# An involution loop in steps of two tile rows, with longer runs of each kind of matmul and the norm parameters in other PSUM buffers

## The chip, the cores and the metric

The kernel runs on one core of one Trainium2 chip. The metric is the device time in microseconds (us), as the median of several executions; the three of the kernel before lie between 2418.53 and 2431.75 us. Times inside an execution come from one profiled execution, whose span is 2421.5 us. PE is TensorE, DVE VectorE, ACT ScalarE, POOL GpSimd and SP SyncE, which here issues the DMAs.

## The reference, cut to what matters

The input is x, 8 images of 256 channels and 56 x 56 pixels, in float32. Two layers follow each other, each with a residual:

```python
x = x + involution(group_norm(x))            # layer 0
x = x + ternary_conv_block(group_norm(x))    # layer 1

def involution(x):                           # K = 7, 16 groups
    ker = w_span @ (w_reduce @ x + b_reduce) + b_span    # per pixel: 16 groups x 49 taps
    out[c, y, x] = sum over the 49 taps of ker[group of c, tap, y, x] * x_padded[c, y + ky, x + kx]
```

Layer 1 makes ternary weights of w1 and w2, and does convolution, batch norm, relu, convolution, batch norm, a sum and a relu. The change touches layer 0 alone.

## The kernel before, in words

**Stages.** A start-up of about 205 us loads the weights, quantizes the weights of layer 1 and prepares image 0. Then comes the loop of the involution, to 1244 us. Two convolution phases follow, and a last stage that sums and stores.

**Tiling of the involution.** An image is cut into 4 quarters of 64 channels (`quarters`, 32 in all); the two halves of the image's height lie on partitions 0 to 63 and 64 to 127. A half is 10 tile rows of 7 tiles, and a tile is 3 x 8 pixels (the tenth row has one line of pixels, so 8 instead of 24). For each tile the 49 taps are written as a matrix from the 9 x 14 = 126 pixels around it to its 24 pixels, and the involution of the tile is a matmul with that matrix. So three kinds of PE work belong to a tile row:

- *Application*, `apply_row` (L704, tile `pa`): 28 fp32 matmuls of 32 columns, each of which the profile shows as 2, so 56. `pick_out` then takes the result out of PSUM: ACT (L716), DVE (L717), and POOL adds it to x (L720).
- *Matrices*, `generate` (L671, tile `pg`): a quarter needs 14 units, each for 2 to 4 of the 24 pixel places and two groups (`UNITS`; 8 to 16 matmuls in the profile). A unit takes one tile of the pool `ps_p`, which has 2 buffers of two banks. Units of four places have one or two places taken out by ACT (L675, two calls a place), and DVE takes out the rest (L680), after ACT, because both work on the same PSUM tile. The matrices of quarter m + 1 are made while quarter m is applied.
- *Transposes*, `transpose_q` (L638, tile `ptq`, 3 matmuls): the pixels of three of the row's seven tile columns, normalized by POOL (`surround`), are transposed and copied by ACT (L641) beside the other four, which `load_q` brings from DRAM. Those four were made for the next image in strips (`prep`: POOL, then 4 transposes `pt`, L605, an ACT copy, L608, and a store).

`ptq` and `pt` share 2 PSUM buffers of the pool `ps_a`, and `pa` has 2 more: with the 2 x 2 banks of `ps_p` that is 8 banks.

**Order.** The loop is written out by hand. One turn is one tile row, and `pin` keeps each engine's instructions in the order of the text. A turn issues transfers, `apply_row`, the loads of four rows ahead, the transposes of two rows ahead (`QLEAD`), statistics on DVE, `pick_out`, one or two units of matrices (`PER_ROW`, none in the tenth row), a half step of a strip, and on even rows a part of `surround`.

**Norm parameters.** Once per image, in three turns, `params` makes the group norm's scale and shift of the next image: two small matmuls (`gnp`), a chain of tiny DVE instructions with one ACT square root, a scaled copy of the reducing weights, and 8 small matmuls (`br`). Its PSUM tiles come from `ps_p`, the pool of the matrices. `reduce` (tile `pk`, L538) then applies the reducing weights, in the turns that make the last units of an image.

```python
PER_ROW = (2, 1, 2, 1, 2, 1, 2, 1, 2, 0)
...
        row = apply_row(b, c, a, ty)
        prefetch()
        if m * TY + ty + QLEAD < len(rows):
            transpose_q(*rows[m * TY + ty + QLEAD])
...
        pick_out(b, c, ty, *row)
        for _ in range(PER_ROW[ty]):
            next(gen, None)
```

Of the kernel before, what the change touches and what calls it, by code (L numbers as in the profile page):

```python
# [15 lines left out]
P = 128  # L16
# [62 lines left out]
def involution_tri_block_kernel(  # L79
# [61 lines left out]
    def group_norm_params(mv, dst, psum_tile, name):  # L141


        n = mv.shape[1]
        ps = psum_tile(f"gnp_{name}")
        nc.tensor.matmul(ps[:, :2 * n], grp_sb, mv.rearrange("p n s -> p (n s)"),
                         start=True, stop=True)
        yield
        gm = small.tile([P, n, 2], F32, tag=f"gn_gm{n}", name=f"gm_{name}")
        nc.vector.tensor_copy(gm.rearrange("p n s -> p (n s)"), ps[:, :2 * n])  # L150
        d = small.tile([P, n], F32, tag=f"gn_d{n}", name=f"d_{name}")
        nc.vector.tensor_tensor(d, mv[:, :, 0], gm[:, :, 0], ALU.subtract)
        nc.vector.tensor_tensor(d, d, d, ALU.mult)
        ps2 = psum_tile(f"gnp2_{name}")
        nc.tensor.matmul(ps2[:, :n], grp_sb, d, start=True, stop=True)
# [5 lines left out]
        nc.vector.scalar_tensor_tensor(dst[:, :, 1], gm[:, :, 0], -1.0, rs, ALU.mult, ALU.mult)  # L161
# [273 lines left out]
    with ExitStack() as ph1:  # L435
# [30 lines left out]
        def params(b):  # L466


            dst = small.tile([P, NCQ, 2], F32, tag="gn1", name=f"gn1_{b}")
            yield from group_norm_params(mvs.pop(b), dst, ps_flat, f"a{b}")  # L470
            ps = ps_flat(f"br_{b}")
            for c in range(NCQ):
                nc.vector.tensor_scalar(
                    wrn[:, c, :].rearrange("p (i r) -> p i r", i=2),
                    wr[:, c, :].unsqueeze(1).to_broadcast([P, 2, CR]),
                    dst[:, c, 0:1], None, ALU.mult)
                for i in range(2):
                    nc.tensor.matmul(ps[i * CR:(i + 1) * CR, :1], wr[:CH, c, :], dst[:CH, c, 1:2],
                                     start=(c == 0), stop=(c == NCQ - 1))
# [102 lines left out]
        def prep(b):  # L582

            for c in range(NCQ):
                d = xt_d[b % 2][c][:]

                def store(src, row, o=None, d=d):

                    n = src.shape[0]
                    if o is None:
                        src, to = src.rearrange("p k c -> p (k c)"), [[1, RP]]
                    else:
                        to = [[P, NK], [1, CH]]
                    nc.sync.dma_start(
                        bass.AP(d.tensor, d.offset + row * QX * RP + (o or 0), [[RP, n]] + to), src)

                for s in range(HH // SR):
                    spread(xn, xs[b, c][:, s * SR * W:(s + 1) * SR * W], 0, NK,  # L600
                           prm[b][:, c, 0:1], prm[b][:, c, 1:2])
                    yield
                    pt = ps_a.tile([P, 512], F32, tag="pt", name=f"pt_{b}_{c}_{s}")
                    for k in range(NK):
                        nc.tensor.transpose(pt[:NSP, k * P:(k + 1) * P],  # L605
                                            xn[:, k].rearrange("p r x -> p (r x)"), ident_sb)
                    stg = work.tile([P, NK, P], F32, tag="stg", name=f"stg_{b}_{c}_{s}")
                    nc.scalar.copy(stg[:NSP].rearrange("p k c -> p (k c)"), pt[:NSP, :RP])  # L608
                    tasks.append(lambda stg=stg, s=s: store(stg[:NSP], PAD + s * SR))

                    e = PAD * QX
                    if s == 0:
                        tasks.append(lambda stg=stg: store(stg[:e, :, CH:], PAD + HH, 0))
                    elif s == HH // SR - 1:
                        tasks.append(lambda stg=stg: store(stg[NSP - e:NSP, :, :CH], 0, CH))
                    yield


        tasks = []
# [13 lines left out]

        def transpose_q(b, c, ty):

            pt = ps_a.tile([P, 512], F32, tag="pt", name=f"ptq_{b}_{c}_{ty}")
            for k in range(NX):
                nc.tensor.transpose(  # L638
                    pt[:NQ, k * P:(k + 1) * P],
                    xe[c % 2][:, k, PY * ty:PY * ty + QY].rearrange("p r x -> p (r x)"), ident_sb)  # L640
            nc.scalar.copy(loads[b, c, ty][:NQ, NK:].rearrange("p k c -> p (k c)"),  # L641
                           pt[:NQ, :NX * P])
# [94 lines left out]

        def gn2_stats(b, c, ty):

            if ty == 1:  # L740
# [36 lines left out]
            reduce(0, py)  # L777
        for _ in prep(0):
            transfer(len(tasks))
        apool = ph1.enter_context(tc.tile_pool(name="apool", bufs=1))  # L780

        def matrices(m):
# [11 lines left out]


        quarters = [(b, c) for b in range(B) for c in range(NCQ)]


        X_AT = (0, 1, 4, 5, 7, 8, 14, 15)
        STRIPS_AT = 23  # L800
        for _ in range(NQB):
            prefetch()
        for _ in surround(0, 0):
            pass
        rows = [(b, c, ty) for b, c in quarters for ty in range(TY)]
        for k in rows[:QLEAD]:
            transpose_q(*k)
        pin(start=True)
        last = None
        strips = iter(())  # L810
        for m, (b, c) in enumerate(quarters):
            a = a_next
            gen = iter(())
            if m + 1 < len(quarters):
                a_next = matrices(m + 1)
                gen = generate(*quarters[m + 1], a_next)
                around = surround(*quarters[m + 1])
            more = b + 1 < B
            for ty in range(TY):
                r = c * TY + ty  # L820

                if last is not None and ty in (2, 3):
                    store_x1(*last, ty - 2)
                elif more and r in X_AT:
                    load_x(b + 1, X_AT.index(r) // 2, X_AT.index(r) % 2)
# [7 lines left out]
                if more and r >= 20:  # L833
                    if r == 20:
                        norm = params(b + 1)
                    next(norm, None)
                if ty == 1 and last is not None:
                    gn2_stats(*last, TY)
                elif ty >= 2:
                    gn2_stats(b, c, ty - 1)  # L840
                if more and 4 <= r < 20:
                    gn1_stats(b + 1, (r - 4) // NCB, (r - 4) % NCB)
# [3 lines left out]
                if more and r == STRIPS_AT:  # L846
                    strips = prep(b + 1)
# [121 lines left out]
```

## Time and profile before

| | |
|---|---|
| device time, median of 3 | 2423.54 us |
| PE busy in the profiled execution | 1885.9 us (78%) |
| DVE busy | 1671.0 us (69%) |
| ACT busy | 1261.0 us (52%) |
| POOL busy | 592.9 us (24%) |
| involution loop | 205 to 1244 us |
| its `pg`, `pa`, `ptq` matmuls (L671, L704, L638) | 460.9, 270.4 and 178.6 us busy |

A line of groups in the profile gives the source line, the engine and operation, what is written and read with its shape, the number of instructions, busy time, the mean of one, and the engine's idle time just before them with what ended most of it. Matmuls overlap, so their busy times are longer than the distance between their starts. A "timeline" lists merged runs of instructions: start, duration, engine, line, operation, count, and in brackets the idle time before with its releaser. "issue" there is idle time for which the profile shows no awaited event.

### The profile page before, as it was taken

Reading aid. Unit: us, or ns where it says so; the run is one execution under the profiler, and the core shown is the slowest. Engines: PE = TensorE matmul, PEld = TensorE weight load, DVE = VectorE, ACT = ScalarE, POOL = GpSimd, SP = SyncE. Lnnn points to the kernel's source line nnn. Section 1 sums busy time; section 2 is a strip of 40 time slices with the busy share of each in tenths; the row PEclk is TensorE's granted clock in tenths of the full one; section 3 lists DMA queues with packets and bytes.
Section 4 is the critical chain, followed back from the end, with each engine's and each line's share of the span. In section 5 each row is a group of like instructions: output and inputs, shape, how many; then the busy total and the mean of one; then the engine's idle time right before and its main releaser. Section 6 shows DMA issues by size and latency. Waiting matters only on the chain.

```text
span 2421.5 us, 72092 instructions
## 1 busy us (share of the span) xinstructions
PE 1885.9 (78%) x31080; PEld 1711.2 (71%) x31080; DVE 1671.0 (69%) x2570; ACT 1261.0 (52%) x2404; POOL 592.9 (24%) x1325
## 2 busy tenths in 40 slices
PE   3419898989899898989968999999499999980000
PEld 2217777777777777777858999999499999980000
DVE  6277465564746466574649999999599999974444
ACT  1105454545545454555645667666466677653333
POOL 2404463545546364554630000000000000000000
PEclk8559999999999999999988999999799999995555
DMA  4426363654636364553553233222432233229998
GB/s 155 152 99 177 106 198 109 182 151 144 187 110 206 90 198 137 160 173 107 161 185 149 109 132 137 112 109 106 176 123 109 109 136 136 109 111 430 430 430 377
DMA packets 124441, 406.46 MB, mean 168 GB/s; under 512 B 25694, under 2 KB 32220, under 8 KB 115420
## 3 DMA queue, kind: packets, MB, share of 16 engines
q1 hardware_dynamic: 117664, 360.89, 43.5%
q10 hardware_dynamic: 6460, 40.97, 4.2%
q8 instruction: 244, 4.00, 0.7%
q14 instruction: 73, 0.60, 0.1%
HBM read 259.33 MB, written 142.48 MB: 166 GB/s over the span
## 4 chain that ended last, share of the span: by engine, by line
PE 41%; DMA 10%; DVE 2%; ACT 1%; issue 1%; SPq 0%; POOL 0%; ACTq 0%; DVEq 0%
PE c L388 35%; DMA y1f<-y1d 3%; PE pg L671 3%; DMA out_y<-x1f 2%; DMA x1f<-x1d 2%; PE pa L704 2%; DVE x1f L899 1%; PE ptq L638 1%; DMA y2f<-y2d 1%; DMA y1d<-y 1%; DMA wq<-wqd 1%; PE pk L538 0%; PE pt L605 0%; ACT a L675 0%; DVE a L680 0%
## 5 line engine op out<-in xcount | busy, mean ns | idle before, releaser
L388 PE MATMUL c<-pl,wq 128*128 128x392 f32 x4608 | 857.3, 348 | 51.3 <-ACT pl L294 32.0
L388 PEld LDWEIGHTS c<-pl,wq 128*128 128x128 f32 x4608 | 855.4, 189 | 53.1 <-ACT pl L294 32.8
L680 DVE TENSOR_TENSOR a<-pg,bt 126x756 f32<-126x756 f32 (+3 forms) x640 | 393.8, 656 | 283.2 <-ACT a L675 225.7
L671 PE MATMUL pg<-kr,wl 64*126 64x140 f32 (+1 forms) x6144 | 460.9, 293 | 56.8 <-DVE a L680 32.5
L671 PEld LDWEIGHTS pg<-kr,wl 64*126 64x126 f32 x6144 | 394.8, 194 | 112.0 <-issue 70.3
L704 PE MATMUL pa<-a,q 126*32 126x48 f32 x17920 | 270.4, 208 | 71.5 <-DMA q<-xtd 44.5
L641 ACT COPY q<-ptq 126x384 f32<-126x384 f32 x320 | 153.0, 478 | 314.0 <-issue 171.0
L675 ACT ACTIVATE a<-pg,bt 126x126 f32<-126x126 f32 x768 | 242.5, 475 | 136.0 <-PE pg L671 136.0
L704 PEld LDWEIGHTS pa<-a,q 126*32 126x32 f32 x17920 | 221.7, 111 | 128.5 <-issue 89.4
L720 POOL TENSOR_TENSOR x<-x,inv 128x168 f32<-128x168 f32 x320 | 165.5, 517 | 577.4 <-DVE inv L717 557.0
L717 DVE SCALAR_TENSOR_TENSOR inv<-pa,half_sb,inv 128x168 f32<-128x168 f32 x320 | 118.6, 371 | 213.3 <-ACT inv L716 212.2
L294 ACT CAST pl<-r 128x812 fp32r<-128x812 f32 x192 | 162.4, 867 | 153.0 <-DVE r L289 136.4
L351 ACT ACTIVATE dummy<-y,nc 128x1568 f32<-128x1568 f32 x128 | 205.3, 1604 | 15.6 <-DVE y L374 14.3
L295 DVE TENSOR_TENSOR pl<-r,pl 128x812 fp32r<-128x812 f32 x192 | 186.3, 996 | 30.6 <-ACT pl L294 29.7
L275 POOL MEMSET xp<- 128x116 f32 x32 | 6.3, 196 | 817.7 <-DVE a L289 817.6
L561 POOL TENSOR_SCALAR xn<-x,gn 128x224 f32<-128x224 f32 (+2 forms) x384 | 184.2, 500 | 29.1 <-PE pt L605 18.5
L638 PE MATMUL ptq<-ident_sb,xe 128*126 128x128 f32 x960 | 178.6, 296 | 9.4 <-ACT stg L608 7.0
L561 POOL TENSOR_SCALAR xe<-x,gn 128x168 f32<-128x168 f32 (+2 forms) x384 | 160.3, 437 | 19.9 <-DVE gn L161 19.9
L139 DVE BATCH_NORM_STATS2 st<-x 128x6 f32<-128x392 f32 x256 | 138.0, 555 | 9.9 <-DMA x<-in_x 9.3
L608 ACT COPY stg<-pt 98x512 f32<-98x512 f32 x128 | 79.9, 624 | 122.0 <-PE pt L605 61.6
L716 ACT ACTIVATE inv<-pa,half_sb 128x168 f32<-128x168 f32 x320 | 126.9, 397 | 1.9 <-PE pa L704 1.8
L638 PEld LDWEIGHTS ptq<-ident_sb,xe 128*126 128x126 f32 x960 | 101.3, 143 | 29.7 <-ACT stg L608 7.2
(134 smaller groups left out, 1740.2 us busy)
## 6 DMA issues: line engine op xcount, KB each, us to landing
q<-xtd SPq DMA_DIRECT2D x320, 252.0 KB
raw<-x1d SPq DMA_DIRECT2D x32, 812.0 KB
raw<-y1d SPq DMA_DIRECT2D x32, 812.0 KB
x<-in_x SPq DMA_DIRECT2D x64, 392.0 KB
xtd<-stg SPq DMA_DIRECT2D x128, 196.0 KB
x1d<-x SPq DMA_DIRECT2D x64, 392.0 KB
y1d<-y SPq DMA_DIRECT2D x32, 784.0 KB
y2d<-y SPq DMA_DIRECT2D x32, 784.0 KB
```

Source lines behind the costliest of these rows:

```text
L294: nc.scalar.copy(hi, r)
L295: nc.vector.tensor_tensor(lo, r, hi.bitcast(F32), ALU.subtract)
L351: nc.scalar.activation(dummy, y[:, to], f, bias=shift[:, to:to + 1], accum_out=stats[:, to, j, n:n + 1])
L388: nc.tensor.matmul(ps[:, to, :NM], wq[:, k, t, dx, to * P:(to + 1) * P], part[:, t, :, dx:dx + W], start=(c == 0), stop=(c == last))
L561: nc.gpsimd.tensor_scalar(dst[:, i - d - k0:f - d - k0, :, x0:x0 + n], v[:, i:f, :, j0:j0 + n], scale, bias, ALU.mult, ALU.add)
L638: nc.tensor.transpose(pt[:NQ, k * P:(k + 1) * P], xe[c % 2][:, k, PY * ty:PY * ty + QY].rearrange("p r x -> p (r x)"), ident_sb)
L641: nc.scalar.copy(loads[b, c, ty][:NQ, NK:].rearrange("p k c -> p (k c)"), pt[:NQ, :NX * P])
L671: nc.tensor.matmul(dst, wl[rows, c, gp, o:o + NQ], kr[py][rows, px, :], start=True, stop=True)
L675: nc.scalar.activation(whole[:, g0 + i, p0 + j], ps[:NQ, i, j * nt:(j + 1) * nt], AF.Identity, bias=bt[:, c, g0 + i, p0 + j:p0 + j + 1])
L680: nc.vector.tensor_tensor(dst[:, g0:g0 + 2, p0:p0 + nv].rearrange("q g p t -> q g t p"), ps[:NQ, :, t0 * nv:t1 * nv].rearrange("q i (t p) ...
L704: nc.tensor.matmul(ps[o:o + 32, k * 2 * n:(k + 1) * 2 * n], q[:NQ, k, o:o + 32], av[:, t + k, g * 2 * n:(g + 1) * 2 * n], start=True, stop ...
L720: nc.gpsimd.tensor_tensor(xv, xv, iv.rearrange("p t (y x) -> p y t x", x=PX), ALU.add)
```

## The change

A turn of the loop becomes a step of two tile rows. In a step PE first applies both rows, then makes three units of matrices (two in the fifth step of a quarter, `PER_STEP`), then does the transposes of two rows, now four rows ahead, and then those of a strip. So each kind of matmul comes in a run twice as long, and PE changes between kinds less often, which is what it is for. `pick_out` of both rows, DVE's statistics and the loads move with it; a strip is now one turn of its generator and not two.

The norm parameters take their PSUM tiles from the two buffers of the transposes (`ps_one`) and not from those of the matrices, and `params` is cut into six parts, two to a step, so that a part's DVE work stands behind the step's other DVE work. The buffer counts of all pools stay as they were, and so do all instructions of layer 1.

```diff
-PER_ROW = (2, 1, 2, 1, 2, 1, 2, 1, 2, 0)
+PER_STEP = (3, 3, 3, 3, 2)
+NS = len(PER_STEP)
 NQB = 4
-QLEAD = 2
...
         nc.vector.tensor_tensor(d, d, d, ALU.mult)
+        yield
         ps2 = psum_tile(f"gnp2_{name}")
...
+        def ps_one(name):
+            return ps_a.tile([P, 512], F32, tag="pt", name=name)
...
-            yield from group_norm_params(mvs.pop(b), dst, ps_flat, f"a{b}")
-            ps = ps_flat(f"br_{b}")
+            yield from group_norm_params(mvs.pop(b), dst, ps_one, f"a{b}")
             for c in range(NCQ):
                 nc.vector.tensor_scalar(
...
-                for i in range(2):
-                    nc.tensor.matmul(ps[i * CR:(i + 1) * CR, :1], wr[:CH, c, :], dst[:CH, c, 1:2],
-                                     start=(c == 0), stop=(c == NCQ - 1))
...
             prm[b], prm_edge[b] = dst, edge
+            yield
+            ps = ps_one(f"br_{b}")
+            for c in range(NCQ):
+                for i in range(2):
+                    nc.tensor.matmul(ps[i * CR:(i + 1) * CR, :1], wr[:CH, c, :], dst[:CH, c, 1:2],
+                                     start=(c == 0), stop=(c == NCQ - 1))
             yield
...
-            for ty in range(TY):
-                r = c * TY + ty
...
+            for s in range(NS):
+                n = c * NS + s
...
                 transfer(2)
-                row = apply_row(b, c, a, ty)
-                prefetch()
-                if m * TY + ty + QLEAD < len(rows):
-                    transpose_q(*rows[m * TY + ty + QLEAD])
...
+                step = [(ty, apply_row(b, c, a, ty)) for ty in (2 * s, 2 * s + 1)]
+                for _ in step:
+                    prefetch()
...
+                next(norm, None)
...
-                pick_out(b, c, ty, *row)
-                for _ in range(PER_ROW[ty]):
+                for ty, row in step:
+                    pick_out(b, c, ty, *row)
+
+                for _ in range(PER_STEP[s]):
                     next(gen, None)
...
+                for k in rows[(m * NS + s) * 2 + NQB:(m * NS + s) * 2 + NQB + 2]:
+                    transpose_q(*k)
                 next(strips, None)
-                if ty % 2 == 0 and m + 1 < len(quarters):
-                    next(around)
+                for _ in range((2, 2, 1, 0, 0)[s]):
+                    next(around, None)
+                next(norm, None)
                 pin()
```

More of the change, by code (lines that the diff above doesn't have):

```diff
@@ L602, in prep @@
                     yield
-                    pt = ps_a.tile([P, 512], F32, tag="pt", name=f"pt_{b}_{c}_{s}")
+                    pt = ps_one(f"pt_{b}_{c}_{s}")
                     for k in range(NK):
@@ L608, in prep @@
                     nc.scalar.copy(stg[:NSP].rearrange("p k c -> p (k c)"), pt[:NSP, :RP])
[L609 removed]
+                    tasks.append(lambda stg=stg, s=s, store=store: store(stg[:NSP], PAD + s * SR))
                     e = PAD * QX
                     if s == 0:
[L613 removed]
+                        tasks.append(lambda stg=stg, store=store: store(stg[:e, :, CH:], PAD + HH, 0))
                     elif s == HH // SR - 1:
[L615 to L616 removed]
+                        tasks.append(lambda stg=stg, store=store: store(stg[NSP - e:NSP, :, :CH], 0, CH))
         tasks = []
@@ L634, in transpose_q @@
         def transpose_q(b, c, ty):
-            pt = ps_a.tile([P, 512], F32, tag="pt", name=f"ptq_{b}_{c}_{ty}")
+            pt = ps_one(f"ptq_{b}_{c}_{ty}")
             for k in range(NX):
@@ L738, in gn2_stats @@
         def gn2_stats(b, c, ty):
-            if ty == 1:
+            if (b, c) not in gst:
                 gst[b, c] = (small.tile([P, NCB, 6], F32, tag="gn_st2", name=f"st2_{b}_{c}"), 0)
@@ L779, in involution_tri_block_kernel @@
             transfer(len(tasks))
+        transfer(len(tasks))
         apool = ph1.enter_context(tc.tile_pool(name="apool", bufs=1))
@@ L796, in involution_tri_block_kernel @@
         quarters = [(b, c) for b in range(B) for c in range(NCQ)]
-        X_AT = (0, 1, 4, 5, 7, 8, 14, 15)
-        STRIPS_AT = 23
+        rows = [(b, c, ty) for b, c in quarters for ty in range(TY)]
+        STATS_AT, PARAMS_AT, STRIPS_AT = 2, 10, 12
         for _ in range(NQB):
@@ L804, in involution_tri_block_kernel @@
             pass
-        rows = [(b, c, ty) for b, c in quarters for ty in range(TY)]
-        for k in rows[:QLEAD]:
+        for k in rows[:NQB]:
             transpose_q(*k)
@@ L809, in involution_tri_block_kernel @@
         last = None
-        strips = iter(())
+        strips = norm = iter(())
         for m, (b, c) in enumerate(quarters):
             a = a_next
-            gen = iter(())
+            gen = around = iter(())
             if m + 1 < len(quarters):
@@ L818, in involution_tri_block_kernel @@
             more = b + 1 < B
-            for ty in range(TY):
-                r = c * TY + ty
[L822 to L825, printed above, removed]
-                transfer(2)
-                row = apply_row(b, c, a, ty)
-                prefetch()
-                if m * TY + ty + QLEAD < len(rows):
-                    transpose_q(*rows[m * TY + ty + QLEAD])
[L833 to L837, printed above, removed]
-                    gn2_stats(*last, TY)
[L839 to L842, printed above, removed]
-                pick_out(b, c, ty, *row)
-                for _ in range(PER_ROW[ty]):
+            for s in range(NS):
+                n = c * NS + s
+                if more and n == PARAMS_AT:
+                    norm = params(b + 1)
+                if more and n == STRIPS_AT:
+                    strips = prep(b + 1)
+                if more and n < 2 * NCQ:
+                    load_x(b + 1, n // 2, n % 2)
+                transfer(2)
+                step = [(ty, apply_row(b, c, a, ty)) for ty in (2 * s, 2 * s + 1)]
+                for _ in step:
+                    prefetch()
+                if last is not None and s == 0:
+                    for h in range(2):
+                        store_x1(*last, h)
+                next(norm, None)
+                if last is not None and s == 1:
+                    gn2_stats(*last, TY)
+                if s > 0:
+                    gn2_stats(b, c, 2 * s)
+                if more and STATS_AT <= n < STATS_AT + 2 * NCQ:
+                    for j in range(2 * (n - STATS_AT), 2 * (n - STATS_AT) + 2):
+                        gn1_stats(b + 1, j // NCB, j % NCB)
+                for ty, row in step:
+                    pick_out(b, c, ty, *row)
+                for _ in range(PER_STEP[s]):
@@ L845, in involution_tri_block_kernel @@
                     next(gen, None)
-                if more and r == STRIPS_AT:
-                    strips = prep(b + 1)
+                for k in rows[(m * NS + s) * 2 + NQB:(m * NS + s) * 2 + NQB + 2]:
+                    transpose_q(*k)
                 next(strips, None)
-                if ty % 2 == 0 and m + 1 < len(quarters):
-                    next(around)
+                for _ in range((2, 2, 1, 0, 0)[s]):
+                    next(around, None)
+                next(norm, None)
```

## The prediction

> **What bounds the kernel now.** I read the busy time by stretches first. The change touches only the loop of the involution, 205 to 1244 us of the span. Columns: stretch, length, then busy time (and instructions) of PE, PE's weight loads, DVE, ACT, POOL, the granted PE clock, DMA share, GB/s.
>
> ```profile
> 205.00:1244.00 1039.00, 945.19 (x25172) 789.33 (x25162) 611.18 (x1335) 554.80 (x1512) 521.76 (x1189) 0.97 0.51 152
> ```
>
> PE is busy for 91% of the loop, DVE 59%, ACT 53%, POOL 50%: PE sets the pace. The timeline of PE alone shows how. These are two tile rows that make three units of matrices:
>
> ```profile
> 632.58 0.80 PE L704 MATMUL pa<-a,q 126*32 126x48 f32 x56
> 633.31 0.55 PE L638 MATMUL ptq<-ident_sb,xe 128*126 128x128 f32 x3
> 633.79 2.03 PE L671 MATMUL pg<-kr,wl 64*126 64x126 f32 x32
> 635.75 0.65 PE L605 MATMUL pt<-ident_sb,xn 128*98 128x128 f32 x4
> 636.32 0.80 PE L704 MATMUL pa<-a,q 126*32 126x48 f32 x56
> 637.06 0.55 PE L638 MATMUL ptq<-ident_sb,xe 128*126 128x128 f32 x3
> 637.53 1.21 PE L671 MATMUL pg<-kr,wl 64*126 64x126 f32 x16
> 638.67 0.80 PE L704 MATMUL pa<-a,q 126*32 126x48 f32 x56
> ```
>
> No gap stands in brackets: PE runs from start to start, and the two rows take 6.09 us. Compare this with the timeline of all engines elsewhere, which also shows what a unit with two places on ACT costs after PE:
>
> ```profile
> 607.40 1.15 PE L671 MATMUL pg<-kr,wl 64*126 64x126 f32 x16
> ...
> 608.48 0.55 PE L704 MATMUL pa<-a,q 126*32 126x48 f32 x32
> 608.60 1.25 ACT L675 ACTIVATE a<-pg,bt 126x126 f32<-126x126 f32 x4 [0.26 <-PE pg L671]
> ...
> 609.88 0.68 DVE L680 TENSOR_TENSOR a<-pg,bt 126x504 f32<-126x504 f32 x1 [1.12 <-ACT a L675]
> 610.13 0.46 PE L704 MATMUL pa<-a,q 126*32 126x48 f32 x24 [1.10 <-issue]
> ```
>
> 16 `pg` matmuls take 1.08 us to the next start and 32 take 1.96, so 55 to 59 ns each and about 0.14 us for leaving the kind. Leaving `pa` costs 0.13 in the same way (24 take 0.39, 56 take 0.73), leaving transposes 0.07 (0.137 us between two starts, 0.20 to the next kind).
>
> Two losses interrupt this. The last line shows the first: 1.1 us that end with nothing awaited, inside a run of one kind. Listed over the loop, 42 such gaps lie at the same place of a count by 256 PE instructions, 45 us together, about 2.4 us after an instruction packet starts on a queue of its own:
>
> ```profile
> q8 instruction: 244, 4.00, 0.7%
> ```
>
> The second comes once per image, at the norm parameters:
>
> ```profile
> 662.74 0.36 PE L155 MATMUL gnp_a<-d_a,grp_sb 128*128 128x4 f32 x2 [0.60 <-DVE d_a L153]
> ...
> 667.06 0.63 PE L478 MATMUL br<-gn,wr 64*64 64x1 f32 x16 [2.08 <-DVE gn L161]
> ...
> 670.83 2.07 PE L671 MATMUL pg<-kr,wl 64*126 64x126 f32 x16 [2.06 <-DVE a L680]
> 672.83 1.35 PE L704 MATMUL pa<-a,q 126*32 126x48 f32 x56
> ```
>
> With 1.40 us at 659.94 and 1.2 at `pk`, PE waits 7.3 us, and afterwards works slower for a while (the last `pa` takes 1.27 us to the next start, not 0.73), some 1.3 us more. 8.6 us times 7 images is 60 us.
>
> **What the Trainium skill says.** "TensorEngine Tiling (Array Packing)", Key Properties: changing the tiling mode drains the array. The trace agrees, with the 0.07 to 0.14 us above. "PSUM — Partial Sum Buffer", Specifications: 8 banks per partition. The pools take 2 x 2 + 2 + 2 = 8, so a longer run finds no spare buffer; and "Perfetto Trace Analysis", Optimization Strategy, names a gap that repeats on the engine that should be saturated as a sign of too few buffers. No such gap is in the trace of before outside the norm parameters. "Runtime: NRT & Kernel Launch", Instruction fetch mechanics: instructions arrive in blocks of 16 KiB or 256, mostly hidden. The trace agrees on the block (4.00 MB in 244 packets) but shows 45 us that are not hidden.
>
> **The change part by part.** All times are for a quarter that makes matrices (31 of them), unless said.
>
> *Fewer changes of kind.* Before: 10 times out of `pa`, 10 out of `ptq`, 9 out of `pg`; after: 5, 5 and 5, and a strip follows `ptq` in the same kind. Saved: 5 x 0.13 + 5 x 0.07 + 4 x 0.14 = 1.56 us, times 31 is 48 us, and 112 strips times 0.07 is 8 us. Sum: -56 us, all on PE's path.
>
> *A third unit in a row on two buffers.* This wait is new. In the order of the changed kernel, the third `pg` unit of a step waits for DVE's removal of the first. Take the second step (units of 16 matmuls with two, one and two places on ACT), from the first `pa` at 0. Two rows take 1.22, the change of kind 0.13, so the first unit starts at 1.35. From its start to the end of its removal before: 607.40 to 610.56, which is 3.16. So the third unit starts at 1.35 + 3.16 + 0.06 = 4.57, and PE would have wanted it at 1.35 + 2 x 0.94 = 3.22: a wait of 1.35 us. Third step (first unit with one place on ACT, 0.74, and 0.94 on DVE; then two units of 12 matmuls): 1.35 us too. First step (DVE alone, 0.94 + 0.2, but behind DVE's two `pick_out` instructions, which end at 1.22 + 0.26 + 0.41 + 0.39 = 2.3): 0.75. Fourth: 0.4. Fifth: two units, none. Sum 3.85 us, times 31 is +119 us. Before, one or two units stood in a row, and 2.5 us of other PE work hid the removal.
>
> *A strip on two buffers.* The strip's `pt` needs the buffer of the step's first `ptq`, so it waits for ACT's copy of that, which stands in ACT's queue behind the last unit's ACT calls. Second step: third unit ends at 5.5, ACT takes 1.25 from 5.8, then 0.48 for the copy, so `pt` starts near 7.35 where PE was ready at 6.45: 0.9 us. The other steps by the same sum: 0.35, 0.35, 0.35, 0.45. With strips in all five, 2.4 us; there are 112 strips or 22.4 quarters' worth, so +54 us. Behind PE's waiting `pt` stand the next step's rows, and everybody waits for those.
>
> *The norm parameters.* Their waits leave the matrices' buffers, but DVE reads their tiles at the end of a step, and the step's second `ptq` needs that buffer. In the three steps concerned I get 1.2, 2.2 and 2.2 us (in the second DVE ends the last unit at 7.7 where `ptq` wanted 6.1; in the third PE also waits 0.8 for the last norm result, and 16 `br` matmuls take 0.5). 5.6 us replaces 8.6, so -3 x 7 = -21 us.
>
> *Instruction packets.* No instruction is added. A block and PE's queue ahead of it are about the 320 instructions of two rows, which take 5.6 us now when nothing waits. A step with waits takes 6.4 (mean over 112 with strips), so PE asks less often. If the gaps fall off as their mean of 1.08 us suggests, exp(-0.8/1.08) leaves half of 45 us, and some of that hides behind the new waits: I take 17, so -28 us; between 5 and 45 is possible.
>
> *At nothing:* the loads (a row is loaded four rows ahead as before; the ACT copy into it waits for no load of its own step), statistics (DVE has 40% free), POOL (in a step with strip and two parts of `surround` 2 x 0.54 + 1.35 + 2 x 1.25 = 4.9 us of some 6 to 8), and the wait of a quarter's first row for the last matrices, which stays near its 0.5 us.
>
> Sum: -56 + 119 + 54 - 21 - 28 = +68. 2423.5 + 68 gives about **2490 us**.
>
> **The rivals.**
> *A: the longer runs pay.* If the removal of a unit kept up with PE, neither new wait would come. For it speaks that DVE and ACT are little over half busy; against it that the wait is one of latency (3.16 us against 1.88 of PE work), not of load. Then the packets come closer together: at 5.0 us for 320 instructions 45 us become about 70. Time: 2423.5 - 56 - 21 + 25 = 2371.
> *B: the waits come at half size,* because gaps of the packets let DVE and ACT catch up: 68 - 87 = -19 from the waits, but then the packets' gain is lost too (+28): 2432.
> *C: worse.* The packets' gaps stay (+28) and the waits are 15% longer, since DVE's instructions pile up behind POOL and ACT (+26): 2544.
>
> **How the numbers follow.** The forecast gets 0.62: the waits follow from buffer counts and durations that the trace shows. C gets 0.13, B 0.11, A 0.14. Leaving out A and the part of C above 2545 leaves out nearly 2 in 10, so the range is 2425 to 2545. Faster by over 0.5% (under 2411): A and a little of B, 0.15. Within 0.5% (to 2436): most of B, 0.07. Slower: 0.78.
>
> **What would show it.** In the changed profile PE's busy share of the loop falls below 85%, `pg` shows idle time ended by DVE's L684 of some 100 us, `pt` idle time ended by ACT's L645 of some 50 us; the timeline shows `pa` x112 and `ptq` x6 in one piece, with the gap ahead of the last unit of a step; 42 packet gaps become fewer than 25; around the norm parameters no wait above 2.3 us. I am wrong if three units follow each other on PE with no gap, or if a step with a strip takes under 5.6 us.

## The result, and the profile after

The changed kernel takes 2559.93 us (median of 4, 2543.63 to 2568.41) where the kernel before, beside it, took 2421.43 (median of 4). The ratio is 1.0556, with a 95% interval of 1.0493 to 1.0619. It is slower, as forecast, but by 138 us and not by 68, and lies above the forecast's range.

All of it is in the loop of the involution. The last `pa` ends at 1255.4 us before and at 1388.3 after, 133 us later, and the profiled spans differ by the same 133 (2421.5 and 2554.6). The view of stretches for the loop after, with the columns of the line shown before:

```profile
205.00:1372.00 1167.00, 920.53 (x25010) 787.94 (x25010) 620.59 (x1327) 564.65 (x1507) 511.94 (x1179) 0.97 0.45 134
```

PE's busy share falls from 91% to 79% at the same granted clock: the loop got slower because PE waits, not because it computes longer. What for is in the view of waits. First the kernel before, PE alone, over its loop; columns: waiting group, releaser, then us in total, times, longest.

```profile
PE pg L671 <- DVE a L680: 24.5, 15, 2.1
PE br L478 <- DVE gn L161: 14.6, 7, 2.1
PE pg L671 <- issue: 14.4, 18, 1.7
PE pa L704 <- issue: 12.9, 14, 2.1
PE pa L704 <- DVE a L680: 10.2, 24, 0.8
PE pk L538 <- DVE a L680: 8.3, 7, 1.2
```

The same view of the changed kernel:

```profile
PE pg L675 <- DVE a L684: 73.9, 100, 1.2
PE pt L610 <- ACT q L645: 56.4, 109, 0.9
PE pa L708 <- issue: 38.3, 20, 3.0
PE pg L675 <- issue: 35.4, 27, 3.0
PE ptq L642 <- ACT q L645: 16.9, 21, 1.2
PE pk L544 <- DVE a L684: 13.9, 14, 1.2
```

The two PSUM waits of the forecast are the first two lines. The next two were not in it: idle time that ends with nothing awaited has grown from 27.3 to 73.7 us. All of those gaps stand at a boundary of 256 PE instructions, where PE passes from one block of instructions to the next. The timeline of PE shows all three in 13 us (a step begins at each `pa`, 482.74 and 490.60; columns: start, duration, engine, line, operation, count, idle time before with its releaser):

```profile
482.19 0.62 PE L610 MATMUL pt<-ident_sb,xn 128*98 128x128 f32 x4 [0.43 <-ACT q L645]
482.74 1.41 PE L708 MATMUL pa<-a,q 126*32 126x48 f32 x112
484.08 0.50 PE L675 MATMUL pg<-kr,wl 64*126 64x140 f32 x3
485.99 1.57 PE L675 MATMUL pg<-kr,wl 64*126 64x140 f32 x21 [1.41 <-issue]
488.13 0.74 PE L675 MATMUL pg<-kr,wl 64*126 64x140 f32 x8 [0.57 <-DVE a L684]
488.81 0.88 PE L642 MATMUL ptq<-ident_sb,xe 128*126 128x128 f32 x6
490.06 0.62 PE L610 MATMUL pt<-ident_sb,xn 128*98 128x128 f32 x4 [0.38 <-ACT q L645]
490.60 1.14 PE L708 MATMUL pa<-a,q 126*32 126x48 f32 x88
494.73 0.46 PE L708 MATMUL pa<-a,q 126*32 126x48 f32 x24 [2.98 <-issue]
```

The longer runs are there (`pa` x112, `ptq` x6). The third unit waits (488.13), the strip waits (490.06), and two blocks of instructions come late (485.99, 494.73). Counting the gaps by their place, every 256th PE instruction, and taking what each is longer than the usual distance of its two matmuls, the packets of instructions cost 45.4 us in 44 gaps before and 94.2 us in 60 after. That count is used for all runs below, under the name *packet gaps*.

### The profile page after: what moved, and what is told of

It reads as the page before. It is cut to its first block, busy times and chain, and to the rows that moved or that the text cites. A ratio compares the mean times of both kernels' runs of the same rounds, so it can differ in the third digit from the quotient of the medians.

```text
span 2554.6 us, 71992 instructions
## 1 busy us (share of the span) xinstructions
PE 1862.3 (73%) x31080; PEld 1711.6 (67%) x31080; DVE 1683.7 (66%) x2570; ACT 1273.5 (50%) x2404; POOL 587.1 (23%) x1325
## 5 line engine op out<-in xcount | busy, mean ns | idle before, releaser
L708 PE MATMUL pa<-a,q 126*32 126x48 f32 x17920 | 239.6, 209 | 53.8 <-issue 44.3
L708 PEld LDWEIGHTS pa<-a,q 126*32 126x32 f32 x17920 | 214.0, 113 | 85.8 <-issue 73.6
L645 ACT COPY q<-ptq 126x384 f32<-126x384 f32 x320 | 144.4, 499 | 250.5 <-PE ptq L642 103.7
L642 PE MATMUL ptq<-ident_sb,xe 128*126 128x128 f32 x960 | 152.6, 294 | 65.8 <-ACT q L645 58.8
L642 PEld LDWEIGHTS ptq<-ident_sb,xe 128*126 128x126 f32 x960 | 106.9, 146 | 94.3 <-ACT q L645 63.8
L610 PE MATMUL pt<-ident_sb,xn 128*98 128x128 f32 x512 | 86.7, 296 | 95.8 <-ACT q L645 56.4
```

The costliest lines, as they stand in the source:

```text
L642: nc.tensor.transpose(pt[:NQ, k * P:(k + 1) * P], xe[c % 2][:, k, PY * ty:PY * ty + QY].rearrange("p r x -> p (r x)"), ident_sb)
L708: nc.tensor.matmul(ps[o:o + 32, k * 2 * n:(k + 1) * 2 * n], q[:NQ, k, o:o + 32], av[:, t + k, g * 2 * n:(g + 1) * 2 * n], start=True, stop ...
```

## The experiments

Times are medians, and each ratio is against the kernel before, run on the same chip in the same series.

| run | change to which kernel | time, us | ratio, 95% | packet gaps, us |
|---|---|---|---|---|
| e1 | after, third unit behind the transposes | 2466.35 | 1.0166 (1.0129 to 1.0203) | 99 |
| e2 | after, strip behind the application | 2493.51 | 1.0300 (1.0253 to 1.0346) | 46 |
| e3 | before, norm parameters' part alone | 2379.48 | 0.9822 (0.9795 to 0.9848) | 49 |
| e4 | after, loads in mid-step | 2571.88 | 1.0620 (1.0584 to 1.0656) | 100 |
| e5 | after, stores behind loads | 2555.45 | 1.0547 (1.0523 to 1.0572) | 93 |
| e6 | after, no loads | 2529.17 | 1.0447 (1.0428 to 1.0466) | 74 |
| e7 | e1 and e2 together | 2453.38 | 1.0138 (1.0108 to 1.0168) | 68 |
| e8 | e3, strip behind `ptq` | 2376.13 | 0.9803 (0.9783 to 0.9823) | 39 |
| e9 | after, boundaries shifted by 128 | 2538.93 | 1.0482 (1.0424 to 1.0541) | 62 |
| e10 | e2, boundaries shifted by 128 | 2491.38 | 1.0275 (1.0246 to 1.0304) | 49 |
| e11 | after, a unit between the two rows | 2521.11 | 1.0407 (1.0361 to 1.0452) | 83 |
| e12 | after, boundaries shifted by 256 | 2566.98 | 1.0586 (1.0564 to 1.0608) | 100 |
| e13 | after, boundaries shifted by 96 | 2538.09 | 1.0471 (1.0448 to 1.0493) | 71 |

**The two waits, and the norm parameters.** e1 moves the third unit:

```diff
-                for _ in range(PER_STEP[s]):
+                for _ in range(2):
                     next(gen, None)
                 for k in rows[(m * NS + s) * 2 + NQB:(m * NS + s) * 2 + NQB + 2]:
                     transpose_q(*k)
+                for _ in range(PER_STEP[s] - 2):
+                    next(gen, None)
                 next(strips, None)
```

> The changed kernel, with the third unit of a step behind the transposes of the two rows and ahead of the strip's: pa pa, pg pg, ptq ptq, pg, pt. Both new waits lose their cause: between the first and the third unit lie two ptq (about 1.05 us), and between the first ptq and pt a whole unit. It costs about one more change of kind a step (124 x 0.17 = 21 us). Theory W+P (two causes, independent: the waits for buffers cost some 150 us, and the instruction packets come late because the loads start in a burst behind the two pa and the run of short instructions is long): waits fall by about 130, packet gaps stay at 85 to 100 us, so about 2560 - 130 + 21 = 2450 us. Theory S (the packets come late because PE's waits for semaphores keep the queue of instructions ahead of it empty, so the packet gaps are a consequence of the waits): packet gaps fall to 40 or below, about 2400 us. If neither wait was real the time would stay at 2560 or rise to 2580.

Both waits nearly go, `pg` behind DVE from 73.9 to 24.7 us and `pt` behind ACT from 56.4 to 8.3, and 94 us of time with them. So both waits were real, and the packet gaps do not need them, for they stay (99 us): theory S falls, W+P holds, 16 us above its number.

e2 moves only the strip:

```diff
                     prefetch()
+                next(strips, None)
...
                     transpose_q(*k)
-                next(strips, None)
```

> The changed kernel, with the strip's transposes moved from the end of a step to just behind the application of its two rows, ahead of the matrices. pt then takes a buffer whose copy is a step old; the wait of the third unit for DVE stays. The strip wait was put at 54 us in the prediction, and idle time ahead of pt sums to 56 to 72 us in the changed kernel's trace. Two theories: the wait is additive, and the time falls by 50 to 75 us to about 2490 to 2510; or the DVE and ACT queues are what lags and the wait is only passed on to the next step's third unit, the time falls by less than 25 us, and pg's idle time behind L684 rises from 74 us to over 110.

66 us faster, in the band of the first theory. In the view of waits of e2 the line `pt` behind ACT is gone:

```profile
PE pg L675 <- DVE a L684: 111.6, 107, 1.2
PE pa L708 <- DVE a L684: 23.8, 23, 1.0
PE pg L675 <- issue: 22.6, 20, 2.0
PE ptq L642 <- ACT q L645: 16.8, 21, 1.2
PE pk L544 <- DVE a L684: 13.8, 14, 1.2
PE pa L708 <- issue: 9.5, 13, 1.4
```

But the time doesn't come from where that theory had it. Much of the wait did pass on (`pg` behind DVE grew from 73.9 to 111.6 us, `pa` behind DVE from 8.3 to 23.8), as the second theory said, and what makes up for that are the "issue" lines, which fell from 73.7 to 32.1 us. Neither theory had the packets in it. This is the lead that the later runs follow.

e7 adds e1's move to e2.

```diff
                     prefetch()
+                next(strips, None)
...
-                for _ in range(PER_STEP[s]):
+                for _ in range(2):
                     next(gen, None)
...
                     transpose_q(*k)
-                next(strips, None)
+                for _ in range(PER_STEP[s] - 2):
+                    next(gen, None)
```

> e2 (strip behind the application) with the third unit of a step put behind the transposes: pa pa, pt, pg pg, ptq ptq, pg. Against e2 it removes the third unit's wait for DVE and adds a change of kind a step (124 x 0.17 = 21 us). If the third unit costs the 110 us or so that stand as excess inside pg in e2 against e1, the time is 2493 - 105 + 21 = 2410 us, provided the packet gaps stay at e2's 46 us. If they come back to e1's 99 us because blocks are drained faster without waits, about 2460. If the third unit's wait is worth half, about 2455 too, but with packet gaps of 46 in the trace.

2453 us is near the second of the numbers, for neither reason in full: the packet gaps came half way back (68 us), and part of the wait appeared ahead of the third unit behind `ptq` (32 us by the distances between starts). With both PSUM waits cut down, steps of two rows are still 1.4% slower than the kernel before.

e3 makes the second half of the change alone. Its core, on the kernel before:

```diff
-            yield from group_norm_params(mvs.pop(b), dst, ps_flat, f"a{b}")
+            yield from group_norm_params(mvs.pop(b), dst, ps_one, f"a{b}")
...
                     next(gen, None)
...
+                if more and r >= 20:
+                    next(norm, None)
```

> The kernel before (steps of one tile row), with the part on the norm parameters alone: PSUM tiles from the transposes' buffers, and params cut into six parts, two to a turn, one behind the application and one at the turn's end. If this part is worth what its waits cost (7.3 us an image in the trace before, and 1.3 of slower PE after them), 8.6 falls to 3 or 4 us an image, times 7: about 2421 - 35 = 2386 us; with the prediction's 5.6 an image, about 2400. If the waits only move to the transposes, no change, 2421.

2379 us is 43 us less than before and below the lowest of the expected values, 2386. The view of waits shows where: the 24.5 us of `pg` behind DVE before have become 0.3.

```profile
PE pg L677 <- issue: 15.4, 14, 2.7
PE pa L710 <- issue: 13.3, 18, 1.8
PE br L489 <- DVE gn L162: 10.4, 7, 1.5
PE pa L710 <- DVE a L686: 9.4, 22, 0.8
PE pk L544 <- DVE a L686: 8.3, 7, 1.2
PE gnp_a L156 <- DVE d_a L153: 6.3, 7, 0.9
...
PE pg L677 <- DVE a L686: 0.3, 1, 0.3
```

So one half of the change is a gain, and the steps of two rows cost more than the whole loss. e8 goes on from e3, with the strip's turn right behind the row's transposes:

```diff
                     transpose_q(*rows[m * TY + ty + QLEAD])
+                if more and r == STRIPS_AT:
+                    strips = prep(b + 1)
+                next(strips, None)
...
-                if more and r == STRIPS_AT:
-                    strips = prep(b + 1)
-                next(strips, None)
```

> e3 (the kernel before with the norm parameters' part alone) with the strip's turn moved from the end of a turn to just behind the transposes of the row, so that pt follows ptq in one kind. It saves a change of kind per strip (112 x 0.14 = 16 us) and two of its buffers' waits are not in sight: 2379 - 12 = 2367 us. Rival: POOL's 1.35 us for a strip and ACT's copy now stand ahead of the row's pick_out and the units' ACT calls, the removal of units comes later, and the time is 2379 or more.

2376 us: not told apart from e3 by the intervals, though the packet gaps fell by 10 us; 9 us of new waits ahead of `pt` and 10 more inside `pa` took that back.

**Is it DMA traffic that makes the packets late?** A packet starts about 0.8 us after PE passes the boundary when the DMA is idle, and over 3.1 us after it in a tenth of the blocks of the changed kernel; PE then has the instructions some 2.4 us after the packet's start. In the changed kernel the late starts went with DMA traffic: the DMA share in the first microsecond of a block is 0.07 where the packet starts within 0.9 us, and 0.83 where it takes over 2.6. Three runs move the traffic. e4 moves the loads:

```diff
-                for _ in step:
-                    prefetch()
...
-                for _ in range(PER_STEP[s]):
+                for j in range(PER_STEP[s]):
                     next(gen, None)
+                    if j < 2:
+                        prefetch(True)
```

where `prefetch(True)` writes one column of the new tile on DVE ahead of the load, so that the load starts behind it.

> The changed kernel, with the start of the two rows' loads moved: each is held back by a tiny DVE write into its tile behind the first and the second unit of a step, so that the DMA traffic starts in the middle of the step and one row at a time, not in a burst behind the two pa. PE's order is the same. Theory D (packets are late because the burst of loads stands in the DMA rings ahead of them just when the run of 224 short instructions drains a block): packet gaps fall from 85 to some 50 us, time about 2525. Theory R (the run of short instructions alone is to blame, the packet's own latency is just longer than the block): gaps stay at 75 to 95 us, time within 15 us of 2560. The two added DVE writes a step cost DVE about 0.1 us each, at worst 0.2 x 124 = 25 us behind the third unit's wait.

The loads start at 5.05 us of the step instead of 2.09 (medians), and the gaps are 100 us: theory D falls for the burst of loads, R's time fits, with gaps 5 us above its band.

e5 moves the stores:

```diff
-                transfer(2)
                 step = [(ty, apply_row(b, c, a, ty)) for ty in (2 * s, 2 * s + 1)]
                 for _ in step:
                     prefetch()
+                transfer(2)
```

> The changed kernel with one line moved: the strip's store (and the other deferred transfers) is issued behind the loads of the step's two rows, not ahead of them. PE's order and all waits on PSUM buffers are unchanged. In the changed kernel a strip's store starts 0.76 us after the first pa of a step (median), just where the block of instructions with the two pa begins; with the strip moved forward (e2) it starts at 2.9 us and the packet gaps were 46 us instead of 88. Theory St (the store is what delays the packets): packet gaps fall to about 50, time about 2560 - 38 = 2522. Rival L (the loads, or any burst of that size, delay them): gaps 75 to 95, time within 12 us of 2560.

The strips' stores now start 2.55 us into the step, and nothing changes (93 us of gaps, 2555 us): theory St falls.

e6 leaves the loads out:

```diff
-                loads[k] = load_q(*k)
+                if len(qs) < NQB:
+                    qs.append(load_q(*k))
+                    loads[k] = qs[-1]
+                else:
+                    qs.append(qs.pop(0))
+                    loads[k] = qs[-1]
```

> The changed kernel without the loads of tile rows from DRAM: four tiles are loaded at the start and used again and again, so 316 loads of 252 KB are left out and the output is not the reference's. PE's order and its waits on PSUM are unchanged. Theory D (packets are late through DMA traffic): packets start 0.8 to 1.0 us after the block boundary nearly always, and by the blocks' measured lengths 10 to 15 us of gaps remain, with the strips' stores still there perhaps 40: time 2485 to 2515. Rival R (short blocks alone): gaps stay at 75 or more, time 2545 or more. A lower time could also come from rows that waited for their loads; the trace shows almost none of that (8 waits or so).

Between the two: 74 us of gaps are left of 94, so the loads are worth some 20 us of them, and the greater part needs no load.

**Where the boundaries fall.** Without the loads (e6, where the DMA share of the loop is 0.25 and not 0.45) late packets remain, and most of their gaps lie in certain blocks: those in which a strip's `pt` is among the first 60 instructions. In the changed kernel 42 of the 94 us stand there. In such a block the packet starts late (1.1 us after that `pt` began, in the median, with loads and without). In the changed kernel the rest of such a block is the `pt`, the two rows' `pa` and a few `pg`, about 2 us of work, while the next block is there 1.1 + 2.4 = 3.5 us after the `pt` began. PE stands for the difference: 42.3 us in 31 blocks, or 1.36 each. The timeline above has such a block (the `pt` at 482.19 is 17 instructions into it): the packet starts at 483.36, and PE stands until 485.99. Over the loop, from the traces:

| run | blocks with `pt` in the first 60 | mean start of the packet after the boundary, us | packet gaps of these blocks, us |
|---|---|---|---|
| before | 30 | 1.70 | 14.0 |
| after | 31 | 2.59 | 42.3 |
| e2 (`pg` follows the `pt`) | 21 | 1.53 | 0 |
| e11 | 29 | 3.71 | 46.8 |
| e1 | 21 | 3.31 | 47.0 |

Now an image is 6648 PE instructions in the changed kernel, 26 blocks less 8. So the boundaries return to nearly the same place of the loop with each image, and a bad place is met again and again. The step around 512 us is one image after one at 355 and one before 671; its `pt` is 49, then 41, then 33 instructions into its block, and each time the block after it is late:

```profile
515.02 0.61 PE L610 MATMUL pt<-ident_sb,xn 128*98 128x128 f32 x4 [0.43 <-ACT q L645]
515.57 1.23 PE L708 MATMUL pa<-a,q 126*32 126x48 f32 x103
518.38 0.26 PE L708 MATMUL pa<-a,q 126*32 126x16 f32 x9 [1.58 <-issue]
...
673.78 0.61 PE L610 MATMUL pt<-ident_sb,xn 128*98 128x128 f32 x4 [0.42 <-ACT q L645]
674.33 1.26 PE L708 MATMUL pa<-a,q 126*32 126x48 f32 x107
677.44 0.24 PE L708 MATMUL pa<-a,q 126*32 126x16 f32 x5 [1.85 <-issue]
```

In e1 an image is 6656 instructions, exactly 26 blocks, so its 21 early `pt` are three places met seven times each. What its 99 us of gaps would be at other places no run shows, and e7 and e11 were run at one position of the boundaries too.

This can be tried without touching the loop, by instructions ahead of it:

```diff
+        ps = ps_one("shift")
+        for _ in range(32):
+            nc.tensor.matmul(ps[:1, :1], ident_sb[:, :1], ident_sb[:, :1], start=True, stop=True)
         pin(start=True)
```

> The changed kernel with 32 one-element matmuls of ident_sb added once, just ahead of the loop (PE shows each as 4 instructions, so 128 instructions, some 2 to 5 us once), written to a tile nobody reads. Nothing in the loop differs, but every boundary of a block of 256 instructions falls half a block later. In the changed kernel an image is 6648 PE instructions, 26 blocks less 8, so the boundaries return nearly to the same places of the loop image after image (6663 and +7 in the kernel before). Theory A (the 88 us of packet gaps are an accident of where the boundaries fall): gaps move to somewhere between 40 and 130 us, and the time by more than 15 us, either way. Rival G (the gaps belong to the new order, wherever the boundaries fall): gaps 75 to 105 us, time 2550 to 2575.

The gaps fell to 62 us, as theory A allows, but the intervals of the two ratios overlap. So e12 (64 matmuls, one whole block) is the control, and e13 (24 matmuls) a second place, whose effect was counted ahead from the changed kernel's trace.

> e9's control: the changed kernel with 64 one-element matmuls ahead of the loop, 256 PE instructions, so that every boundary falls in the loop just where it falls in the changed kernel. Theory B (where the boundaries fall matters: the strip's pt stands among the first 60 instructions of 31 blocks in the changed kernel, 20 in e9): packet gaps of 85 to 100 us and 2555 to 2570 us as in the changed kernel. Rival N (e9's lower gaps were noise between executions, or came from the added matmuls themselves): gaps as in e9, 62 us, time near 2540.

> The changed kernel with 24 one-element matmuls ahead of the loop: 96 PE instructions. Counted in the changed kernel's trace, the strip's pt would then stand among the first 60 instructions of 22 blocks, not 31. Theory B: each of these blocks costs 1.36 us of gap in the changed kernel and 0.99 in e9, so 9 fewer are worth some 10 to 20 us: packet gaps of 60 to 80 us, time 2535 to 2550. Rival N2 (only a shift of just half a block happened to help): gaps 88 to 100 us, time 2555 to 2570.

The control behaves as the changed kernel does (2567 us, gaps 100), and the shift by 96 gives 2538 us, with intervals far apart. Theory B holds: about 29 us of the control's time lie in the place of the boundaries alone. The views of waits of e12, then of e13; the "issue" lines sum to 76.3 and 51.6 us, and the PSUM waits are the same within 5 us:

```profile
PE pg L675 <- DVE a L684: 75.8, 100, 1.2
PE pt L610 <- ACT q L645: 54.2, 108, 1.0
PE pg L675 <- issue: 38.3, 25, 4.3
PE pa L708 <- issue: 38.0, 22, 4.0
```

```profile
PE pg L675 <- DVE a L684: 80.0, 105, 1.3
PE pt L610 <- ACT q L645: 57.9, 112, 0.9
PE pa L708 <- issue: 29.9, 20, 3.7
PE pg L675 <- issue: 21.7, 19, 3.2
```

In e13 the `pt` stood early in 24 blocks (22 were counted ahead), in e9 in 20.

> e2 (the changed kernel with the strip behind the application) with the same 128 PE instructions ahead of the loop. e2's gaps were 46 us, and its boundaries return to the same places but for one instruction an image, so 26 places recur seven times. Theory A: e2's low gaps were luck of the places, and come back to 75 us or more, time about 2525. Rival G: the wait of pt ahead of the run of pa is what made the packets late, its removal is what helped, and gaps stay at 35 to 60 us, time 2485 to 2510.

In e2 the same shift changes nothing (49 us of gaps, 2491 us): with `pg` behind the `pt`, its low gaps are no luck of the place.

**Short blocks, or the strip ahead of them?** e11 cuts the run of `pa` and leaves the strip where it was:

```diff
-                step = [(ty, apply_row(b, c, a, ty)) for ty in (2 * s, 2 * s + 1)]
-                for _ in step:
-                    prefetch()
+                step = [(2 * s, apply_row(b, c, a, 2 * s))]
+                prefetch()
+                next(gen, None)
+                step.append((2 * s + 1, apply_row(b, c, a, 2 * s + 1)))
+                prefetch()
...
-                for _ in range(PER_STEP[s]):
+                for _ in range(PER_STEP[s] - 1):
                     next(gen, None)
```

> The changed kernel with the first unit of matrices of a step put between the applications of its two rows: pa, pg, pa, pg pg, ptq ptq, pt. The run of 224 short instructions is cut in two of 112, as before the change, so that no block of 256 lasts under some 3.4 us; the strip still waits for ACT ahead of the next pa. Theory R (the short blocks make the packets late): packet gaps fall from 94 to 55 us or less. Rival S (the wait of pt ahead of pa does it): gaps stay at 75 or more. Besides, the third unit's wait shrinks by the 0.6 us of the second row in each of four steps (75 us fall to 10 to 25), and a change of kind a step more costs 124 x 0.17 = 21 us. So R: 2560 - 55 + 21 - 40 = about 2486 us; S: about 2526 us.

2521 us is near S's number, 2526. The third unit's wait is gone, as both expected, and the gaps are still 83 us. The waits of e11:

```profile
PE pa L708 <- issue: 66.7, 44, 4.4
PE pt L610 <- ACT q L645: 50.7, 98, 1.0
...
PE pg L675 <- DVE a L684: 7.2, 32, 0.5
```

So the length of the run is not the whole cause; the strip ahead of it seems to count, as far as one position of the boundaries can tell. But S was put too narrowly: in e1 the `pt` hardly waits, and its early blocks are just as late (the table above). Nor is it the `pt` as such, for in the kernel before and in e2 the packets of such blocks start at 1.70 and 1.53 us.

The traces show one more difference. PE's stream also holds separate semaphore instructions, records named EVENT_SEMAPHORE that the views leave out. In the changed kernel one stands directly ahead of every early `pt`, and so it is in e11; in the kernel before none does, and in e2 three of 21. Nor does it take a `pt`. Among the blocks of all fifteen traces without an early `pt`, 140 have such an instruction among the first 50 and later than 0.8 us into the block: there the packet starts 2.7 us after the boundary (median). In 340 others none stands there and the first 50 instructions take over 1.5 us, so that they begin as slowly: there it is 1.1 us. Of these, the blocks with DMA traffic in their first microsecond have 2.7 and 1.4 us. So a late packet goes with a separate semaphore instruction early in the block. It isn't the only thing that does: seven of e1's 21 have none, and their packets start 2.8 us or later, at a DMA share of 0.80 or more in their first microsecond. None of the runs varied this alone, and why a packet is held is not settled here.

## Why the prediction was wrong

The direction was right, and of five steps four were about right. To compare with them, the distances between the starts of consecutive matmuls were summed by pairs of kinds, each as what it exceeds the usual distance of that pair. The differences of the sums add up to the loop's 133 us. They depend on what is taken as usual: with the median or the lower quartile of each pair, single rows move by up to some 11 us.

| step | forecast, us | measured, us | from |
|---|---|---|---|
| fewer changes of kind | -56 | -69 | the sum of usual distances, 701.5 to 632.5 |
| third unit | +119 | +113 | excess inside `pg`, 148.8 in e3 (where no norm parameter holds it up) to 261.9 |
| strip | +54 | +72 | excess ahead of `pt`, none before |
| norm parameters | -21 | -26 | `pg` 186.4 to 148.8 by e3; `ptq`, `br`, `gnp` and `pk` together +12; e3 alone gained 43 |
| instruction packets | -28 | +49 | 45.4 to 94.2 |
| rest | 0 | -6 | inside `pa` and `pk` |

*The step that failed* is the fifth, "PE asks less often", with "a block and PE's queue ahead of it are about the 320 instructions of two rows". It took a mean where the cost comes from single blocks, and it counted a queue of PE ahead of the block, which no line of the trace had shown. The mean time of a block, without its gap, did grow as I said, from 5.04 to 5.51 us. But the quickest got quicker: the quickest tenth went from under 3.67 to under 2.94 us, because a block can now hold both rows' 224 `pa` instructions and little else. And a packet needs some 0.8 us to start and 2.4 to arrive, about 3.2 together, from the boundary and not from 64 instructions ahead of it. So fewer than 256 instructions of PE work must hide it, and behind a strip's `pt` fewer still.

Blocks sorted by the work that they hold, gaps left out, show where the growth lies; this count gives 44 us of gaps before and 90 after:

| blocks | before: number, gaps in us | after: number, gaps in us |
|---|---|---|
| under 3.2 us of work | 6, 5.5 | 23, 35.0 |
| longer, with a `pt` in the first 60 | 30, 14.7 | 28, 38.6 |
| longer, without | 164, 24.2 | 149, 16.9 |

In the changed kernel each of the 23 short blocks was over before the next one had come. So short blocks and those with an early `pt` hold the whole growth, while the many ordinary blocks did gain a little, as forecast.

Of the 77 us by which the packets missed their forecast (-28 to +49) the runs show three parts, which overlap: about 29 us are the place of the boundaries (e12 against e13), 20 us the traffic of the loads (e6), and in e2, where `pg` and not `pa` follows the `pt`, 48 us of gaps are gone. The other steps together were forecast at +96 us and came to +84, so the direction was no luck.

The Trainium skill's "Runtime: NRT & Kernel Launch", Instruction fetch mechanics, has the next block fetched while the current one is executed. That fits: one block is all the lead there is, and I had read it as more. Its "mostly hidden" doesn't hold for this loop, with 94 us of the 1183 from 205 us to its end.

*Rival C* had "packets' gaps stay (+28)", which is the nearest of the cases, and still too low: no case let the gaps grow except A, which had them grow to 70 us only if no wait came. That the waits and the gaps could grow together was left out, and the range ended at 2545 for that reason.

*The signs* that the prediction named: PE's busy share under 85% (79%), some 100 us ahead of `pg` (73.9 as idle time, 113 by starts, since the ends of matmuls are modelled), some 50 ahead of `pt` (56.4), and runs in one piece, all came. No wait around the norm parameters exceeded 2.3 us. "42 packet gaps become fewer than 25" was the one that failed: there were 60.

## What to carry to other kernels

A longer run of one kind saves the changes of kind (69 us here), but with the same PSUM buffers it asks for its third buffer before the first is free. Count the latency of emptying a buffer against the work that stands between its uses, as the forecast did (119 us for the third unit, 113 measured), and put other work between (e1). When PE runs through 256 instructions in about the time that a packet takes, look at the quickest blocks and not at the mean, and at what stands at the head of them. Two versions of such a loop differ by the accident of their instruction count, so shift the count by some instructions ahead of the loop before putting 1% down to the change. Test the parts of a combined change alone: here the norm parameters' part beats both kernels by itself (e3, 1.8% faster than before).

## What the hardware showed beyond that

A kernel with the same loop, instruction for instruction, took 2567 us or 2538 us depending on whether 256 or 96 PE instructions stood ahead of the loop. Where packets started within 0.9 us of the boundary the DMA share was 0.07 in the mean, and where they took over 2.6 us it was 0.83; but leaving out the loads of tile rows took away a fifth of the gaps only. A separate semaphore instruction of PE early in a block went with a late packet, also where no strip's transpose stood there (2.7 us against 1.1).
